# Both 3x3 convolutions of a Mamba-and-residual-block kernel computed on pairs of rows, six products a tile in place of nine

## The chip, the cores and the metric

The kernel runs on one core of a Trainium2 chip. The metric is device time in microseconds (us) of one launch. Before the change three runs gave 27951.63 us (median), 27945.47 and 27972.2. The profile is of one further execution, which took 27950.59 us, with a span of 27948.8 us from its first to its last instruction.

## The reference

Input `x` has 8 images of 64 channels and 128 x 128 points, in float32. Layer 0 runs a two-way Mamba block over all rows and over all columns, averages the two, normalises in groups, and adds `x`. Layer 1 is a residual block with two 3x3 convolutions whose weights are a mixture:

```
# layer 0
xr = run_bidir(rows of x); xc = run_bidir(columns of x)
x1 = silu(group_norm(0.5 * (xr + xc))) + x
# layer 1
w1 = (origin[0:K] + einsum('i,if->f', new_param, P[:, 0:K])).reshape(64, 64, 3, 3)
c1 = relu(batchnorm(conv3x3(x1, w1)))            # batch norm over all 8 images
w2 = (new_param[39] * origin[K:2K] + einsum(... P[:, K:2K])).reshape(64, 64, 3, 3)
out = relu(batchnorm(conv3x3(c1, w2)) + x1)
```

Both batch norms need the statistics of the whole batch before one point can be normalised, so the work falls into three parts with a hard border between them.

## The kernel before

**Layout.** An image lies on 128 partitions as two halves: partitions 0 to 63 hold the 64 channels of rows 0 to 63, partitions 64 to 127 those of rows 64 to 127. A tile is N = 512 points, 4 rows (`SEQ`) of both halves; an image has NT = 16 tiles.

**Part 1, the Mamba loop** (lines 511 to 576) is recorded by hand (`manual_schedule`): each engine's order is the order of the calls. It has 512 groups (8 images, 32 row groups and then 32 column groups each) of 16 slots; `s` counts slots, `n` groups, `r` is the slot in the group, and n % 64 the place in the image. Each slot has a scan on DVE (lines 368 and 370), a product with `c` on POOL (line 375), a drive product on DVE or, in 5 of 16 slots, POOL (line 360), and PE's products `pb` (340) and `yp` (391). Four generators are advanced by one step at fixed slots: `prepare` (the next group), `emit`, `normalize` (421 to 438) and `conv1` (453 to 478).

`normalize` handles an image in the 16 groups after it: a piece of 512 points a group, in slots 5 and 7. For a piece ACT takes the Silu, SP loads `xr`, POOL adds, and SP stores to `x1_d`.

`conv1` reads `x1_d` back. `strip_of` loads a strip of 6 rows on all 128 partitions into one of two buffers, for the tile after the one in work. A tile has nine products of a 128 x 128 weight, which holds the same 64 x 64 block for both halves and zeros elsewhere. It has five steps: three products in each of slots 14, 15 and 0, then in slot 1 the copy out of PSUM (ACT) and the store to `c1_d` (SP), and in slot 2 the statistics (DVE). The first strip is asked for in slot 12 of the group with n % 64 = 4, two slots ahead of its products. The tiles go 1 to 15 and then 0, since tile 0 needs the last row of the other half. The last image has no group after it, so the rest of `normalize` and then the whole of `conv1` run by themselves after the loop (lines 573 to 576):

```
for _ in norm:
    pass
for _ in conv3:
    pass
```

SP is one queue in order: it issues nearly all loads and stores, and an instruction that waits holds up those behind it.

**Part 2, the second convolution** (lines 586 to 636) is placed by the scheduler of the Tile layer. First it clears two image buffers (622), joins the statistics (593) and forms scale and shift. For each image four pieces of 16 rows are loaded to `ct` (ACT's queue), and ACT writes relu(scale x + shift) into `xp` (632). `halo` copies one row each way between the halves by DMA (600, 601), and 8 pairs of tiles of 2 x 9 products each follow (610), with statistics (614), a copy (616) and a store to `c2_d` (617).

**Part 3** (lines 643 to 651) adds `x1` to the normalised result and writes `out`.

Ahead of all this, lines 153 to 160 lay the mixed weights into `w1` and `w2s` with two DMAs each; `w2s` goes to `w2_d`, and only then do the first loads of the image (line 220) start.

Of the kernel before, what the change touches and what calls it, by code (L numbers as in the profile page):

```python
# [32 lines left out]
def tile_mamba2d_then_resblock(ctx: ExitStack, tc: tile.TileContext, x, par, gn, p_w, o_w, new_p, bn, cst, out):  # L33
# [10 lines left out]
    w2_d = dram.tile([P, 9, P], F32, name="w2_d")  # L44
# [12 lines left out]
    w1 = const.tile([P, 9, P], F32, name="w1")  # L57
# [6 lines left out]
    with tc.tile_pool(name="prep", bufs=2) as prep, tc.tile_pool(name="prep_ps", bufs=2, space=PSUM) as prep_ps:  # L64
# [88 lines left out]
        w2s = prep.tile([P, 9, P], F32, name="w2s", bufs=1)  # L153
        for k, w in enumerate((w1, w2s)):
            nc.vector.memset(w, 0.0)
            for hf in range(2):
                nc.sync.dma_start(
                    out=w[hf * C : (hf + 1) * C, :, hf * C : (hf + 1) * C], in_=wacc[k * C : (k + 1) * C]
                )
# [36 lines left out]
    with ExitStack() as st:  # L196
# [12 lines left out]
        for k in range(2):  # L209
            strip = big.tile([P, SEQ + 2, W + 2], F32, name=f"strip{k}")  # L210
            nc.vector.memset(strip, 0.0)
            strips.append(strip)
# [227 lines left out]
        def strip_of(b, t):  # L440
            x1 = x1_d[b].rearrange("p (h w) -> p h w", w=W)
            strip = strips[t % 2]
            lo, hi = max(SEQ * t - 1, 0), min(SEQ * (t + 1) + 1, HH)
            nc.sync.dma_start(out=strip[:, lo - SEQ * t + 1 : hi - SEQ * t + 1, 1 : W + 1], in_=x1[:, lo:hi, :])

            if t == 0:
                nc.vector.memset(strip[0:C, 0, :], 0.0)
                nc.sync.dma_start(out=strip[C:P, 0, 1 : W + 1], in_=x1[0:C, HH - 1, :])
            if t == NT - 1:
                nc.vector.memset(strip[C:P, SEQ + 1, :], 0.0)  # L450
                nc.sync.dma_start(out=strip[0:C, SEQ + 1, 1 : W + 1], in_=x1[C:P, 0, :])

        def conv1(b):


            strip_of(b, 1)
            st1 = small.tile([P, NT, 6], F32, name="st1", bufs=1)
            yield
            for t in [*range(1, NT), 0]:
                if t:  # L460
                    strip_of(b, (t + 1) % NT)
                ps = psm.tile([P, 2, N], F32, name="cps", tag="pt")[:, 0, :]
                for k in range(9):
                    kh, kw = divmod(k, 3)
                    nc.tensor.matmul(  # L465
                        ps.rearrange("p (r w) -> p r w", w=W), w1[:, k, :],
                        strips[t % 2][:, kh : kh + SEQ, kw : kw + W], start=(k == 0), stop=(k == 8),
                    )
                    if k % 3 == 2:
                        yield  # L470
                cs = work.tile([P, N], F32, name="cs", tag="tok", bufs=3)
                nc.scalar.copy(cs, ps)
                nc.sync.dma_start(out=c1_d[b][:, t * N : (t + 1) * N], in_=cs)
                yield
                nc.vector.bn_stats(st1[:, t, :], cs)
                if t == 0:
                    nc.sync.dma_start(out=st1_d[:, b], in_=st1)
                yield
# [32 lines left out]
        with tc.manual_schedule():  # L511
# [10 lines left out]
            for s in range(total + UN):  # L522
# [23 lines left out]
                if r in CONV and n % PER > 4 or r >= CONV[0] and n % PER == 4:  # L546
                    next(conv3, None)
# [10 lines left out]
                if r == OUT and prev:  # L558
                    if n % PER == 4:
                        next(conv3, None)  # L560
# [12 lines left out]
            for _ in norm:  # L573
                pass
            for _ in conv3:
                pass


    with ExitStack() as st:
# [6 lines left out]
        w2 = big.tile([P, 9, P], F32, name="w2")  # L586
# [11 lines left out]
        def halo(xp):  # L598

            nc.sync.dma_start(out=xp[0:C, HH + 1, 1 : W + 1], in_=xp[C:P, 1, 1 : W + 1])  # L600
            nc.scalar.dma_start(out=xp[C:P, 0, 1 : W + 1], in_=xp[0:C, HH, 1 : W + 1])

        def conv3x3(xp, w, stats, dst):
            for t in range(0, NT, 2):
                ps = psw.tile([P, 2, N], F32, name="cps")
                for j in range(2):
                    for k in range(9):
                        kh, kw = divmod(k, 3)
                        r = SEQ * (t + j) + kh
                        nc.tensor.matmul(  # L610
                            ps[:, j, :].rearrange("p (r w) -> p r w", w=W), w[:, k, :],
                            xp[:, r : r + SEQ, kw : kw + W], start=(k == 0), stop=(k == 8),
                        )
                    nc.vector.bn_stats(stats[:, t + j, :], ps[:, j, :])  # L614
                cs = stage.tile([P, 2 * N], F32, name="cs")
                nc.scalar.copy(cs, ps.rearrange("p j n -> p (j n)"))
                nc.sync.dma_start(out=dst[:, t * N : (t + 2) * N], in_=cs)

        xps = []
        for k in range(2):  # L620
            xp = big.tile([P, HH + 2, W + 2], F32, name=f"xp{k}")
# [4 lines left out]
        for b in range(B):  # L626
            xp = xps[b % 2]
            cb = c1_d[b].rearrange("p (h w) -> p h w", w=W)
            for k in range(4):
                ct = stage.tile([P, RB, W], F32, name="ct")  # L630
                nc.scalar.dma_start(out=ct, in_=cb[:, k * RB : (k + 1) * RB, :])
                nc.scalar.activation(  # L632
                    xp[:, 1 + k * RB : 1 + (k + 1) * RB, 1 : W + 1], ct, AF.Relu, bias=t, scale=s
                )
            halo(xp)
            conv3x3(xp, w2, st2[:, b], c2_d[b])
# [76 lines left out]
```

## Time and profile before

Times in us from the span's start, as the profile has them.

| what | us |
|---|---|
| execution that was profiled | 27950.59 |
| its span | 27948.8 |
| first scan of part 1 starts | 120.77 |
| first piece of the last image's norm: POOL adds | 26437.03 |
| last piece of it is stored | 26511.19 |
| first product of its `conv1` | 26515.38 |
| last `c1_d` store issued | 26656.00 |
| first write into `xp` | 26682.85 |
| first product of part 2 | 26695.67 |
| first write of part 3's result, `cc`, on DVE | 27708.77 |

Over the whole span DVE is busy 93%, POOL 90%, PE 71% and ACT 66%. These shares are those of part 1, which is 95% of the span; part 2 and part 3 have other limits.

A line of the groups of instructions reads: line, engine, operation, output<-inputs, shape, count | busy us, mean ns of one | idle us of that engine just before, and what ended most of it. A float32 product is recorded as two instructions here: 8 x 16 x 9 = 1152 products stand as x2304.

### The profile page before, as it was taken

The numbers are of one execution on the slowest core, as the hardware profiler recorded it, in microseconds if no ns is written. First come the engines' busy times: TensorE is split into PE (matmuls) and PEld (weight loads), VectorE is DVE, ScalarE is ACT, GpSimd is POOL, SyncE is SP. The second block draws the span as 40 slices with busy tenths as digits, with TensorE's granted clock in tenths as the row PEclk, the third lists the DMA queues.
The fourth block names the chain that finished last, engine by engine and source line by source line (L and its number), as shares of the span: only waits on it lengthen the run. The fifth ranks groups of instructions, "written<-read, shape, count | busy, mean of one in ns | idle before, by whom it ended". The sixth has DMA issues, their size and how long they took to land. (4 is left out here: it accounts for less than half of the span.)

```text
span 27948.8 us, 235723 instructions
## 1 busy us (share of the span) xinstructions
PE 19978.3 (71%) x66604; PEld 7011.9 (25%) x66604; DVE 26017.8 (93%) x16145; ACT 18328.2 (66%) x30622; POOL 25127.4 (90%) x10916
## 2 busy tenths in 40 slices
PE   6666677666876677666776667766786667766696
PEld 1122222222222222222222222222222222222232
DVE  8999999999999999999999999999999999999811
ACT  5666666666666666666666666666666666666511
POOL 7999999999999999999999999999999999999800
PEclk8888888888988888888888888888898888888798
DMA  5555555555555555555555555555555555555424
GB/s 177 177 174 169 181 185 181 172 169 180 193 176 171 171 184 188 176 168 180 182 184 174 169 182 186 179 172 170 183 191 176 170 175 183 187 177 170 160 81 164
DMA packets 1817540, 4880.91 MB, mean 175 GB/s; under 512 B 236688, under 2 KB 335648, under 8 KB 1799840
## 3 DMA queue, kind: packets, MB, share of 16 engines
q1 hardware_dynamic: 1796144, 4763.96, 51.3%
q10 hardware_dynamic: 15472, 68.32, 0.7%
q0 software_dynamic: 4608, 33.56, 0.3%
q8 instruction: 525, 8.60, 0.1%
q14 instruction: 791, 6.48, 0.1%
HBM read 4124.63 MB, written 739.18 MB: 174 GB/s over the span
## 5 line engine op out<-in xcount | busy, mean ns | idle before, releaser
L375 POOL TENSOR_TENSOR s<-s,c 128x1024 f32<-128x1024 f32 x8192 | 19117.8, 2364 | 1008.3 <-DVE s L370 354.7
L351 ACT ACTIVATE dA<-dl,A 128x508 f32<-128x508 f32 x16384 | 11275.1, 688 | 568.4 <-DMA dl<-dd 52.6
L340 PE MATMUL pb<-u,wb 128*128 128x512 f32 x8192 | 5396.9, 746 | 7362.9 <-DVE s L360 7019.2
L370 DVE TENSOR_TENSOR_SCAN s<-dA,s 128x1024 f32<-128x1024 f32 x4096 | 9295.8, 2280 | 53.9 <-ACT dA L351 40.6
L368 DVE TENSOR_TENSOR_SCAN s<-dA,s 128x1024 f32<-128x1024 f32 x4096 | 9286.9, 2278 | 0.0
L360 DVE TENSOR_TENSOR s<-du,pb 128x1024 f32<-128x1024 f32 x5632 | 6757.1, 1200 | 473.8 <-DMA du<-dd 338.3
L360 POOL TENSOR_TENSOR s<-du,bt 128x1024 f32<-128x1024 f32 x2560 | 6054.9, 2365 | 326.7 <-DMA bt<-bd 127.9
L348 ACT COPY dA<-zeros 128x8 f32<-128x8 f32 x8192 | 1349.0, 165 | 6284.0 <-DVE s L370 4603.6
L391 PE MATMUL yp<-s,fold 128*32 128x512 f32 x32768 | 5388.8, 672 | 5.1 <-POOL s L375 5.1
L340 PEld LDWEIGHTS pb<-u,wb 128*128 128x128 f32 x8192 | 1483.3, 216 | 10217.8 <-DVE s L360 5203.8
L234 PE MATMUL cp<-xc,wc 128*128 128x256 f32 (+3 forms) x8192 | 2151.1, 408 | 0.0
L228 PE MATMUL cp<-xt,wc 128*128 128x512 f32 (+3 forms) x4096 | 2026.2, 618 | 73.7 <-DMA xt<-x_h 73.5
L234 PEld LDWEIGHTS cp<-xc,wc 128*128 128x128 f32 x8192 | 1647.6, 207 | 1071.8 <-issue 459.6
L391 PEld LDWEIGHTS yp<-s,fold 128*32 128x32 f32 x32768 | 820.1, 114 | 3438.6 <-issue 1923.5
L288 PE MATMUL bp<-u,xpT 128*32 128x512 f32 x2048 | 1632.3, 947 | 4.8 <-ACT dl L282 4.8
L351 ACT ACT_TABLE_LOAD x1030 | 1321.5, 1283 | 21.4 <-DMA dl<-dd 3.5
L651 POOL DMA_DIRECT2D out<-cc x32 | 17.2, 537 | 1414.7 <-ACT cc L650 1414.7
L465 PE MATMUL cps<-strip,w 128*128 128x512 f32 x2304 | 1077.2, 606 | 170.7 <-DMA strip<-x_d 160.5
L228 PEld LDWEIGHTS cp<-xt,wc 128*128 128x128 f32 x4096 | 768.7, 198 | 1377.1 <-issue 1089.7
L266 PE MATMUL dp<-u,wd 128*128 128x512 f32 x2048 | 1035.9, 631 | 1.2 <-ACT u L259 1.2
L610 PE MATMUL cps<-xp,w 128*128 128x512 f32 x2304 | 1004.2, 596 | 17.0 <-DMA xp<-xp 16.2
L292 ACT COPY bc<-bp 32x1024 f32<-32x1024 f32 x512 | 513.0, 1002 | 740.4 <-PE yp L391 709.8
(106 smaller groups left out, 10679.9 us busy)
## 6 DMA issues: line engine op xcount, KB each, us to landing
c<-bd SPq DMA_DIRECT2D x2049, 512.0 KB, 4.7
dl<-dd SPq DMA_DIRECT2D x2048, 512.0 KB, 6.4
du<-dd SPq DMA_DIRECT2D x2048, 512.0 KB, 7.3
bt<-bd SPq DMA_DIRECT2D x2560, 256.0 KB, 4.7
dd<-du SPq DMA_DIRECT2D x2048, 128.0 KB, 2.3
dd<-dl SPq DMA_DIRECT2D x2048, 128.0 KB, 2.4
bd<-bc SPq DMA_DIRECT2D x512, 128.0 KB, 5.4
strip<-x_d SPq DMA_DIRECT2D x112, 384.0 KB, 9.5
```

Source lines behind the costliest of these rows:

```text
L228: nc.tensor.matmul(ps[:, :, lo:hi], lhsT[hf], xt[:, r : r + SEQ, lo - s : hi - s], start=start, stop=stop)
L234: nc.tensor.matmul(ps[:, :, lo:hi], lhsT[hf], g["xc"][:, :, lo - s - hf * HH : hi - s - hf * HH], start=start and hf == 0, stop=stop and h ...
L288: nc.tensor.matmul(bp[0 : 2 * NS, d, :], w["wbc"], u[:, d, :], start=True, stop=True)
L340: nc.tensor.matmul(pb, wt[g["o"]]["wb"][:, P * ng : P * (ng + 1)], g["u"][:, d, :], start=True, stop=True)
L348: nc.scalar.copy(dA[:, :, :, edge], zeros)
L351: nc.scalar.activation(dA[:, j, :, t], dl[:, j, :, t], AF.Exp, scale=wt[g["o"]]["A"][:, 2 * half + j, ng : ng + 1])
L360: engine.tensor_mul(s, g["du", half, d], b.unsqueeze(1).to_broadcast([P, 2, N]))
L368: nc.vector.tensor_tensor_scan(s, a, s, 0.0, ALU.mult, ALU.add)
L370: nc.vector.tensor_tensor_scan(s[:, ::-1], a[:, ::-1], s[:, ::-1], 0.0, ALU.mult, ALU.add)
L375: nc.gpsimd.tensor_mul(s, s, c.unsqueeze(1).to_broadcast([P, 2, N]))
L391: nc.tensor.matmul(g["yp"][32 * q : 32 * (q + 1), :], fold, s[:, j, :], start=False, stop=r == UN - 2, skip_group_check=True,)
L465: nc.tensor.matmul(ps.rearrange("p (r w) -> p r w", w=W), w1[:, k, :], strips[t % 2][:, kh : kh + SEQ, kw : kw + W], start=(k == 0), stop= ...
```

## The change

Both convolutions now work on pairs of rows: partitions 0 to 63 hold the even row of each pair and partitions 64 to 127 the odd row, for the output; for the input the two lie one row apart. An output pair then needs two input pairs (`blk` 0 and 1) and three shifts across (`kw`): six products, with three of the four 64 x 64 blocks of each weight in use.

The weights are laid by six DMAs each in place of two. A strip is 5 rows on each half of the partitions, taken from every second row of `x1_d`, by two DMAs (three where the rows cross from one half of the image to the other). `conv1` starts one group later (n % 64 = 5), takes the tiles in an order that follows the pieces of the norm, and does two products in each of its three steps. For the last image five pieces of the norm come first, then one piece and one tile in turn. In part 2 `halo` is gone; `xp` has 65 rows, the first and the last piece are written in halves of 64 partitions, and the result is put back into the old layout by two stores for each pair of tiles, in runs of one row.

```diff
-        w2s = prep.tile([P, 9, P], F32, name="w2s", bufs=1)
+        w2s = prep.tile([P, 2, 3, P], F32, name="w2s", bufs=1)
         for k, w in enumerate((w1, w2s)):
             nc.vector.memset(w, 0.0)
-            for hf in range(2):
-                nc.sync.dma_start(
-                    out=w[hf * C : (hf + 1) * C, :, hf * C : (hf + 1) * C], in_=wacc[k * C : (k + 1) * C]
-                )
+            for blk in range(2):
+                for e in range(2):
+                    for m in range(2):
+                        kh = 2 * blk - e - m + 1
+                        if 0 <= kh < 3:
+                            nc.sync.dma_start(
+                                out=w[e * C : (e + 1) * C, blk, :, m * C : (m + 1) * C],
+                                in_=wacc[k * C : (k + 1) * C, 3 * kh : 3 * kh + 3, :],
+                            )
...
-        def strip_of(b, t):
+        def strip_of(b, t, k):
...
+            for e in range(2):
+                es = slice(e * C, (e + 1) * C)
+                rows = [2 * SEQ * t + 2 * j - e for j in range(SEQ + 1)]
+                for hf in range(2):
+                    js = [j for j, r in enumerate(rows) if hf * HH <= r < (hf + 1) * HH]
+                    if js:
+                        r = rows[js[0]] - hf * HH
+                        nc.sync.dma_start(
+                            out=strip[es, js[0] : js[-1] + 1, 1 : W + 1],
+                            in_=x1[hf * C : (hf + 1) * C, r : r + 2 * len(js) - 1 : 2, :],
+                        )
...
-            strip_of(b, 1)
+            order = [0, 1, 9, 2, 10, 3, 11, 4, 12, 5, 13, 6, 14, 7, 15, 8]
+            strip_of(b, order[0], 0)
...
-            for t in [*range(1, NT), 0]:
-                if t:
-                    strip_of(b, (t + 1) % NT)
+            for k, t in enumerate(order):
+                if k + 1 < NT:
+                    strip_of(b, order[k + 1], k + 1)
...
-                for k in range(9):
...
+                for kw in range(3):
+                    for blk in range(2):
+                        nc.tensor.matmul(
+                            ps.rearrange("p (r w) -> p r w", w=W), w1[:, blk, kw, :],
+                            strips[k % 2][:, blk : blk + SEQ, kw : kw + W],
+                            start=(kw == 0 and blk == 0), stop=(kw == 2 and blk == 1),
+                        )
+                    yield
...
-                if r in CONV and n % PER > 4 or r >= CONV[0] and n % PER == 4:
+                if r in CONV and n % PER > 5 or r >= CONV[0] and n % PER == 5:
                     next(conv3, None)
...
-            for _ in norm:
-                pass
-            for _ in conv3:
-                pass
+            for _ in range(2 * 5):
+                next(norm)
+            next(conv3)
+            for _ in range(NT):
+                for _ in range(2):
+                    next(norm, None)
+                for _ in range(5):
+                    next(conv3)
...
-            for k in range(4):
+            for k in range(0, HH + 1, RB):
                 ct = stage.tile([P, RB, W], F32, name="ct")
-                nc.scalar.dma_start(out=ct, in_=cb[:, k * RB : (k + 1) * RB, :])
...
+                for e in range(2):
+                    es = slice(e * C, (e + 1) * C)
+                    lo, hi = max(k, e), min(k + RB, HH + e)
+                    if lo < hi:
+                        nc.scalar.dma_start(out=ct[es, lo - k : hi - k, :], in_=cb[es, lo - e : hi - e, :])
+                        if k == 0 or k == HH:
+                            nc.scalar.activation(
+                                xp[es, lo:hi, 1 : W + 1], ct[es, lo - k : hi - k, :], AF.Relu, bias=t[es], scale=s[es]
+                            )
+                if 0 < k < HH:
+                    nc.scalar.activation(xp[:, k : k + RB, 1 : W + 1], ct, AF.Relu, bias=t, scale=s)
-            halo(xp)
-            conv3x3(xp, w2, st2[:, b], c2_d[b])
+            for k in range(0, NT, 2):
+                ps = psw.tile([P, 2, N], F32, name="cps")
+                for j in range(2):
+                    for kw in range(3):
+                        for blk in range(2):
+                            r = SEQ * (k + j) + blk
+                            nc.tensor.matmul(
+                                ps[:, j, :].rearrange("p (r w) -> p r w", w=W), w2[:, blk, kw, :],
+                                xp[:, r : r + SEQ, kw : kw + W],
+                                start=(kw == 0 and blk == 0), stop=(kw == 2 and blk == 1),
+                            )
...
+                hf, j0 = divmod(SEQ * k, HH // 2)
+                for e in range(2):
+                    nc.sync.dma_start(
+                        out=c2v[hf, :, j0 : j0 + 2 * SEQ, e, :],
+                        in_=cs[e * C : (e + 1) * C].rearrange("p (j w) -> p j w", w=W),
+                    )
```

## The prediction

> **What bounds the kernel now.** I read the chain that ended last first. It is followed back only to 26665 us, so it says nothing of part 1, but it shows what part 2 is made of: one unbroken run of products, from the halo copy to the statistics.
>
> ```profile
> 26682.85 2.45 ACT xp L632 x2
> 26685.30 1.53 issue
> 26686.83 0.13 ACT xp L632
> 26686.96 6.35 DMA ct<-c_d
> 26693.31 0.02 issue
> 26693.33 0.02 ACT xp L632
> 26693.36 0.32 issue
> 26693.67 1.86 DMA xp<-xp
> 26695.53 0.14 issue
> 26695.67 996.22 PE cps L610 x2286
> ```
>
> Each row is start, us, what. The last row is PE's, 0.436 us a record (996.22 / 2286), and the rows above it are the way there: relu pieces, a late `ct` load, the halo copy. The groups of instructions confirm it, and show where the first convolution stands:
>
> ```profile
> L465 PE MATMUL cps<-strip,w 128*128 128x512 f32 x2304 | 1077.2, 606 | 170.7 <-DMA strip<-x_d 160.5 <-ACT cs L472 10.3
> L610 PE MATMUL cps<-xp,w 128*128 128x512 f32 x2304 | 1004.2, 596 | 17.0 <-DMA xp<-xp 16.2 <-DVE st L614 0.8
> ```
>
> L610 is busy 1004.2 us and idle 17.0, of which 16.2 came before the first product: part 2 is PE's alone. L465 waited 160.5 us for strips, in 8 waits (list of waits): one for each image, 81.3 us of it for the last image, which waits for its norm; the other seven take 79.2 us, 11.3 each.
>
> Part 1 is not PE's. In the table by stretches, groups of the second image without convolution or norm (4473.29 to 5028.11) have DVE busy 541.41 of 554.82 us and POOL 534.67. The timelines of one first strip show the exception:
>
> ```profile
> 3628.21 1.12 PE L340 MATMUL pb<-u,wb 128*128 128x512 f32 x2 [0.68 <-ACT sz L303]
> 3639.86 4.37 PE L465 MATMUL cps<-strip,w 128*128 128x512 f32 x6 [10.53 <-DMA strip<-x_d]
> 3644.16 1.07 PE L391 MATMUL yp<-s,fold 128*32 128x512 f32 x8
> 3645.16 2.84 PE L465 MATMUL cps<-strip,w 128*128 128x512 f32 x6
> 3647.84 1.02 PE L340 MATMUL pb<-u,wb 128*128 128x512 f32 x2
> 3648.69 2.74 PE L465 MATMUL cps<-strip,w 128*128 128x512 f32 x6
> ```
>
> PE stands 10.53 us before the first product; `pb` is behind it, and DVE waits 9.82 us for that `pb` and 2.33 for the next (its timeline), 12.15 for the image.
>
> The tail of part 1, the last image alone, is two chains in a row. SP's timeline (the last two norm pieces, then the first strips) and PE's:
>
> ```profile
> 26506.62 0.32 SPq L437 DMA_DIRECT2D x_d<-xr  x1
> 26507.03 0.38 SPq L434 DMA_DIRECT2D xr<-x_h  x1
> 26511.19 0.32 SPq L437 DMA_DIRECT2D x_d<-xr  x1
> 26511.56 1.10 SPq L444 DMA_DIRECT2D strip<-x_d  x2
> ...
> 26515.38 9.82 PE L465 MATMUL cps<-strip,w 128*128 128x512 f32 x18 [81.26 <-DMA strip<-x_d]
> 26525.92 7.99 PE L465 MATMUL cps<-strip,w 128*128 128x512 f32 x18 [0.72 <-ACT cs L472]
> ```
>
> A store waits for its add and holds the next load back; the strips come when the last piece is out, and only then does PE start.
>
> **The change, part by part.**
>
> *Second convolution, products.* 8 x 16 x 6 x 2 = 1536 records in place of 2304, at the measured 0.436 us (1004.2 / 2304): **-334.7**. A product has the same 512 columns and its own weight load, so its price stays. Is PE still last? A pair of tiles will take 24 x 0.436 = 10.5 us. DVE needs 2 x 0.70 (L614). ACT needs 1.01 (L616) and an eighth of an image's pieces; 3 full ones at 2.10, two of 64 partitions with as many elements, one of a row: about 10.7 / 8 = 1.3. The ten loads of `ct` add some 0.4 us of issue each, 0.5 a pair; 2.9 in all. If ACT also stood out the 4.9 us to landing of each of five pieces it would be 6.0. SP's two stores of 256 KB move in runs of 512 bytes. No such store is in the trace; the nearest row is the strip load, 384 KB in pieces of 512 bytes, which came 3.8 us after its issue in the quiet tail. Two stores in 10.5 us fit; below zero there is nothing to gain, so 0.
>
> *Way into part 2.* The first product now needs only the first piece of `xp`, two half-partition writes of 2.1 and 2.0 us after 26682.85, 4.1 us, where it took 12.8 (26695.67 less 26682.85): **-8.7**. The halo's DMAs were on that path and go; nothing replaces them.
>
> *Tail of part 1.* Before: norm to 26511.19, strip, then 16 tiles, last store at 26656.00. A norm piece takes 4.7 us (SP issues `xr`, POOL adds 3.0 after that, 1.26, SP stores and issues the next); a tile takes 8.67 (7.99 and 0.68 for the copy, as PSUM has one buffer here). After: five pieces, stored by 26459.8 as before; two strips issued from 26460.1; first product 3.8 later. The first tile takes 12 x 0.444 = 5.3 and 1.8 for a cold start (9.82 against 7.99 now), its store is at 26471.7. From then on SP holds, in order, load of piece k+5, its store, two strip loads for tile k+1, store of tile k. So a load of `xr` waits for the tile before, and a strip for the add: 0.4 + 3.0 + 1.3 + 0.4 (store) + 0.4 + 3.6 (two strips, landing) + 5.3 + 0.7 = 15.1 us. The strip it fetches is for the tile after next, so 15.1 us bring two tiles: 7.55 each. Ten tiles to 26547.2, then five without norm at 5.3 + 0.7 = 6.0: 26577.2. Against 26656.0: **-78.8**. Everything from there to 26682.85 (clearing, joining statistics) keeps its length; 65 rows for 66 give 0.2. The new order moves `ct` loads behind the last copy on ACT's queue, but 27 us of DVE hide their landing.
>
> [...] The row: the granted clock was 0.50 in 26450 to 26500, with PE idle, and 1.00 from 26550 (table by stretches); the first tile took 1.8 us more than the next. [...] In the 15.1 us PE is idle 15.1 - 10.7 = 4.4, once 0.7 and once 3.7. [...] I take 0 and keep 10 for the range.
>
> *First strips of the other seven images.* These stay: still asked for in slot 12, used in slot 14. A second strip DMA is issued 0.6 us later (rows of SP near 3632): +0.6. But the products in the way of the two late `pb` shrink by a third: 4.37, 2.84 and 2.74 give back 1.5 + 0.9 + 0.9. -2.7 an image, **-19** for seven.
>
> *Other convolution groups.* By the stretches of the second to fourth image, norm groups with convolution (places 6 to 16) take 52.01, 51.69 and 52.20 us, without it (2 to 4) 51.65, 52.12 and 51.68; places 17 to 20 take 51.01, 51.16 and 51.31, later ones 50.44, 50.47 and 50.27. So convolution costs 0.15 and 0.77 a group, 11 x 0.15 + 4 x 0.77 = 4.7 an image, 33 for seven. PE's third of it would be 11; but SP gets one more issue of 0.6 us in slot 14, ahead of a `bt` load; behind stand the next slots' loads of `c`, for which POOL waits (284.7 us over the span), and the `c1_d` store, which waits for ACT anyway. If that issue came through in full: 112 x 0.6 = +67; if convolution became free, -33. I take **-4**, nearer to the row of POOL and ACT, which PE does not touch.
>
> *Weights.* SP now issues 12 small DMAs where 4 took 2.74 us (0.69 each), and the first image load waits for what follows them: 8 x 0.65 = **+5**. Before 89.44 nothing covers it.
>
> *Part 3* reads and writes what it did: 0.
>
> Sum: -334.7 - 8.7 - 78.8 - 0.2 - 19 - 4 + 5 = -440. On the profiled execution, 27950.6 - 440 = 27510.6; the median of the runs shown lies 1.0 higher, so **27512**.
>
> **Rivals.**
>
> *Tail one after the other* (8%). If the strip comes only for the very next tile, as a wait on the newest store to `x1_d` would make it, each of 11 tiles costs the whole 15.1: +83, the tail gains nothing, 27595. Against: at 26511.56 the old first strip was issued 0.37 after the last piece's store began; it did not wait for that store.
>
> *Another engine takes over part 2* (7%). ACT's loads and writes are in one order with its copies. If they take 12.5 us a pair in place of 10.5, 64 pairs add 130: 27640. For: ACT stood up to 13.9 us for PE in part 2 (list of waits). Against: 2.9 to 6.0 us of work in 10.5.
>
> *First strips hidden or convolution free* (4%): 12.15 - 2.7 = 9.5 more for each of seven images, about -66: 27446. Nothing in the order speaks for it.
>
> *Slower* (3%). Place: PE's queue in slot 14 of every convolution group. If two strip DMAs behind busy loads landed after their slot, every tile would stand as the first does now. Price: 9.5 us (12.15 - 2.7) x 105 further tiles = +997, 28510. It decides from 440 / 112 = 3.9 us a group. For: PE does stand 11.3 us at each first strip. Against: all later strips are asked for a whole group, 51 us, ahead, and land after 9.5 (list of DMA issues).
>
> That the change does not do what it says: six products a tile are in the text, so PE's records must fall; no chance kept.
>
> **How the numbers follow.** 78% for the forecast. Its own bounds: tail +10 for cold starts and some 10 for landings, groups -29 to +71 around my -4, weights 2 less. These do not all fall together, so 27475 to 27575; it holds nearly all of the 78% and, by the first rival's smaller forms, a few more. A change under 0.2% (56 us) cannot be told from none here. Faster 0.96, within 0.2% 0.01, slower 0.03.
>
> **What would show it.** Part 2's products with x1536, about 670 us, idle before the first about 8. `xp` to the first product 4 us. Last `c1_d` store some 140 us after the last norm starts (26437.03), not 219. Waits of PE for strips near 80 us for seven images. Groups of places 6 to 20 within 0.5 us of now. The forecast is wrong if part 2's products show gaps, or if DVE's waits for `pb` grow.

## The result, and the profile after

The changed kernel takes **27639.19 us** (median; 27638.15 to 27651.24), against 27948.74 for the kernel before in the same runs: 309.6 us less, a ratio of 0.9888 with a 95% interval of 0.9871 to 0.9906. The profiled execution took 27638.15 us, its span is 27636.0. The forecast was 27512, with 27575 as its upper end.

The groups of instructions on which the account rests (line, engine, operation, tiles | busy us, mean ns | idle us before them, and what ended it). First two of the kernel before, then three of the changed one:

```profile
L360 DVE TENSOR_TENSOR s<-du,pb 128x1024 f32<-128x1024 f32 x5632 | 6757.1, 1200 | 473.8 <-DMA du<-dd 338.3 <-PE pb L340 103.5 <-PE cp L228 14.0
L375 POOL TENSOR_TENSOR s<-s,c 128x1024 f32<-128x1024 f32 x8192 | 19117.8, 2364 | 1008.3 <-DVE s L370 354.7 <-DVE s L360 320.4 <-DMA c<-bd 284.7
```

```profile
L481 PE MATMUL cps<-strip,w 128*128 128x512 f32 x1536 | 754.4, 618 | 134.3 <-DMA strip<-x_d 128.0
L367 DVE TENSOR_TENSOR s<-du,pb 128x1024 f32<-128x1024 f32 x5632 | 6757.8, 1200 | 559.0 <-DMA du<-dd 452.1
L382 POOL TENSOR_TENSOR s<-s,c 128x1024 f32<-128x1024 f32 x8192 | 19121.0, 2364 | 1104.3 <-DMA c<-bd 440.6
```

The first of these three (line 465 before: 1077.2 us, x2304) has lost a third of its products and some 320 us of busy time; it is the work that the change was made on. The other two are groups that the change does not touch at all, and they tell where time went. DVE's drive products (line 360 before, 367 now) stood 559.0 us where they stood 473.8, and the part ended by a load of `du` rose from 338.3 to 452.1. POOL's wait for `c` (375 before, 382 now) rose from 284.7 to 440.6.

The table by stretches says where. The columns of a row are the stretch, its length, busy time (and records) of PE, PE's weight loads, DVE, ACT and POOL, the granted clock, DMA's share and GB/s. The stretch is places 8 to 16 of the fifth image (a place is the number of a group in its image), nine groups with a piece of the norm and a tile of the convolution each. First the kernel before, then the changed one:

```profile
13684.62:14154.24 469.62, 373.07 (x1170) 119.46 (x1169) 449.58 (x271) 325.52 (x550) 449.77 (x199) 0.90 0.58 192
```

```profile
13715.07:14196.26 481.19, 358.10 (x1116) 109.97 (x1116) 450.03 (x271) 325.45 (x550) 449.95 (x199) 0.89 0.58 186
```

DVE, ACT and POOL do the same work to within half a us; PE does 15 us less; and the stretch is 11.6 us longer. Over seven images such a group takes 53.44 us instead of 52.11, and one of places 17 to 20 takes 51.72 instead of 51.02; later ones are as before (50.25 and 51.24, against 50.35 and 51.21). These groups do less arithmetic and take longer.

The sum, term by term, between two points that both traces have:

| step of the prediction | forecast | measured | from |
|---|---|---|---|
| weights | +5 | +3.9 | first scan, 120.77 to 124.71 |
| first strips, seven images | -19 | -18.3 | the group with the stall, 63.60 to 60.98 |
| other convolution groups | -4 | **+108.1** | places 5, 7 to 20 of seven images |
| rest of the loop | 0 | -5.5 | what is left up to the tail |
| tail | -78.8 | -71.3 | first add to last `c1_d` store, 219.0 to 147.7 |
| way into part 2 | -8.9 | -4.4 | that store to the first product, 39.67 to 35.24 |
| products of part 2 | -334.7 | -328.95 | 1005.01 to 676.06 |
| part 3 | 0 | +3.7 | last product to the end, 248.1 to 251.8 |
| sum | -440 | -312.8 | spans, 27948.8 to 27636.0 |

### The profile page after: what moved, and what is told of

Same layout as the page of the kernel before. It is cut to its first block, busy times and chain, and to the rows that moved or that the text cites. A ratio compares the mean times of both kernels' runs of the same rounds, so it can differ in the third digit from the quotient of the medians.

```text
span 27636.0 us, 232983 instructions
## 1 busy us (share of the span) xinstructions
PE 19347.3 (70%) x65068; PEld 6675.0 (24%) x65068; DVE 26018.6 (94%) x16145; ACT 18349.8 (66%) x30638; POOL 25128.0 (91%) x10916
## 4 chain that ended last, share of the span: by engine, by line
DVE 40%; issue 21%; PE 17%; DMA 10%; ACT 8%; POOL 2%; SPq 1%; DVEq 0%; POOLq 0%; ACTq 0%
DVE s L367 14%; DVE s L375 12%; DVE s L377 10%; DMA du<-dd 7%; PE pb L347 6%; ACT dA L358 4%; PE yp L398 3%; PE cps L650 2%; PE dp L273 2%; PE bp L295 2%; DVE du L287 2%; POOL s L382 1%; DVE y L405 1%; DMA bt<-bd 1%; PE cp L241 1%
## 5 line engine op out<-in xcount | busy, mean ns | idle before, releaser
L382 POOL TENSOR_TENSOR s<-s,c 128x1024 f32<-128x1024 f32 x8192 | 19121.0, 2364 | 1104.3 <-DMA c<-bd 440.6
L367 DVE TENSOR_TENSOR s<-du,pb 128x1024 f32<-128x1024 f32 x5632 | 6757.8, 1200 | 559.0 <-DMA du<-dd 452.1
L241 PE MATMUL cp<-xc,wc 128*128 128x256 f32 (+3 forms) x8192 | 2095.3, 401 | 0.0
L388 PE MATMUL yp<-u,dg 128*128 128x512 f32 x2048 | 961.9, 592 | 1.2 <-DVE y L405 1.2
L481 PE MATMUL cps<-strip,w 128*128 128x512 f32 x1536 | 754.4, 618 | 134.3 <-DMA strip<-x_d 128.0
```

The costliest lines, as they stand in the source:

```text
L241: nc.tensor.matmul(ps[:, :, lo:hi], lhsT[hf], g["xc"][:, :, lo - s - hf * HH : hi - s - hf * HH], start=start and hf == 0, stop=stop and h ...
L367: engine.tensor_mul(s, g["du", half, d], b.unsqueeze(1).to_broadcast([P, 2, N]))
L382: nc.gpsimd.tensor_mul(s, s, c.unsqueeze(1).to_broadcast([P, 2, N]))
```

## The experiments

### What slows the groups

All kernels below but the last two were run once each, and the kernel before, run beside them, took between 27936 and 28022 us. So a total is read to some tens of us, and the argument is carried by the groups (means of 63, in places 8 to 16 of seven images) and by single rows of the traces.

Three theories at first. **A**: the strip's second load is one more issue in SP's queue, which shifts the loads behind it. **B**: its traffic is worse than that of the old strip and slows other loads. **C**: fewer products change PE's timing, and with it the order in which things fall due.

`x1_one_issue` does not load the upper half of the strip; `x2_tiny` issues both loads, of one row each. First the edit of the one, then that of the other:

```diff
-                    if js:
+                    if js and e == 0:
```

```diff
-                    js = [j for j, r in enumerate(rows) if hf * HH <= r < (hf + 1) * HH]
+                    js = [j for j, r in enumerate(rows) if hf * HH <= r < (hf + 1) * HH][:1]
...
-                            in_=x1[hf * C : (hf + 1) * C, r : r + 2 * len(js) - 1 : 2, :],
+                            in_=x1[hf * C : (hf + 1) * C, r : r + 1, :]
```

> The changed kernel, but the strip's half for partitions 64 to 127 is never loaded (that half stays zero), so each strip is one load on SP's queue in place of two, with half the bytes. Read by groups at places 8 to 17 of images 1 to 7 (53.1 us in the changed kernel, 51.9 at places 7 to 16 before). Theory A (the second load on SP's queue[...] makes the du loads late): 51.9, DVE's wait for du back to 1.7 a group. Theory B (the traffic of the row-strided half strips slows the du loads): half of the loss left, 52.5. Theory C (three products fewer change when the other pieces of a group come): 53.1, as in the changed kernel.

> The changed kernel, but each strip load brings one row only (the other rows keep what is in the buffer), so that SP issues as many loads as the changed kernel and the bytes of a strip fall to a fifth. Groups at places 8 to 17: theory A (number of issues) 53.1; theory B (traffic) 51.9 to 52.1; theory C (fewer products) 53.1.

`x1_one_issue` took 27615.76 us, groups 8 to 16 at 52.91: 0.8 of the loss of 1.33 us is left, with half the bytes and one load a strip. `x2_tiny` took 27528.99, those groups at 52.22, DVE's wait for `du` in them at 1.80 us a group (3.11 in the changed kernel, 1.64 before). All issues are there, the loss is not. A falls, B stands.

`x3_before_six` is the kernel before with three of nine products left out; `x4_hybrid` keeps the old first convolution and takes only the new second one, which then reads every second row of the old layout. The main line of the former's edit (the end of the sum and the steps follow it):

```diff
-                for k in range(9):
+                for k in range(6):
...
```

> The kernel before, with the three products of the lowest row of the filter left out of the first convolution: six products a tile in three steps of two, strips and loads as before. Groups at places 7 to 16: theories A and B 51.9 or a little less, DVE's wait for du 1.7 a group; theory C (fewer products) 53.1. The stall at the first strip of an image should shrink from about 11.5 to about 9 us.

> First convolution, its order, its strips and the tail of part 1 as before the change; part 2 as changed, with each row piece loaded from the old layout. All theories: groups at places 7 to 16 at 51.9, last group starts near 26373 us as before, part 2 at 676 us, in all 27948.7 less 329 (products of part 2) less 4 to 8 (way into it): 27612 to 27616. If the loss in part 1 came from anything that part 2 does (it cannot by time, but the pools and orders differ), it would be near 27700.

`x3_before_six` took 27912.33, groups 8 to 16 at 52.05, the one with the first strip at 60.2 instead of 63.6. So C falls, and the 2.7 us an image that I took for the shorter wait of `pb` is seen by itself (3.4). `x4_hybrid` took 27624.96, groups 8 to 16 at 52.12: the loss belongs to the new first convolution, and it eats what that convolution gains at the first strips and in the tail: without it the kernel took 14 us less than the changed one, which one run cannot tell from nothing.

What makes fewer bytes worse traffic? The DMA records of the trace have the time of each packet. The 512-byte packets of a strip took 27.6 ns on average before and 47.6 in the changed kernel, 36.2 in `x1_one_issue` and 27.3 in `x2_tiny`. Two things are new in these loads: every second row of the source (**S**), and two loads of 64 partitions in place of one of 128 (**P**). `x5_contig` is the changed kernel with neighbouring rows; `x6_before_split` is the kernel before with its strip in two loads:

```diff
-                            in_=x1[hf * C : (hf + 1) * C, r : r + 2 * len(js) - 1 : 2, :],
+                            in_=x1[hf * C : (hf + 1) * C, min(r, HH - len(js)) : min(r, HH - len(js)) + len(js), :],
```

```diff
-            nc.sync.dma_start(out=strip[:, ...], in_=x1[:, lo:hi, :])
+            for hs in (slice(0, C), slice(C, P)):
+                nc.sync.dma_start(out=strip[hs, ...], in_=x1[hs, lo:hi, :])
```

> The changed kernel, with one thing different: each half of the pair layout's strip is read as 5 neighbouring rows of the source instead of every second row (the products then work on other rows; sizes, number of loads and the 64-partition halves are as in the changed kernel). Theory S (the row stride at the source is what makes the strip's packets slow): 512-byte packets go back from 47.6 to about 28 ns, groups 8 to 16 of an image from 53.4 to about 52.1 us, the whole to about 27,535 us. Rival P (the split on 64 partitions a load is what slows them): packets stay near 47 ns, groups stay at 53.4 us, the whole at about 27,639 us.

> The kernel before, with each strip loaded by two loads of 64 partitions and 6 neighbouring rows, all 9 products kept. Theory S (row stride): packets stay near 28 ns, groups 8 to 16 stay at 52.1 us, the whole at about 27,949 us. Rival P (split on 64 partitions): packets near 47 ns, groups 8 to 16 at about 53.4 us, the whole some 80 to 100 us longer.

`x5_contig`: packets 47.3 ns, groups 8 to 16 at 53.32, 27665.44 in all. `x6_before_split`: packets **51.1 ns**, groups at **53.59**, 28100.68 in all, 120 above the median of the kernel before beside it (27980.22 in seven runs, the slowest 28021.63). Nothing else was changed in it: same rows, same bytes, nine products. Places 8 to 16 of the fifth image:

```profile
13742.86:14224.87 482.01, 378.17 (x1172) 120.61 (x1171) 449.98 (x271) 325.22 (x550) 449.24 (x199) 0.90 0.59 186
```

482.01 us, where the kernel before has 469.62, by this alone. S falls, P stands. The number of loads is not all of it, since `x1_one_issue` has one load a strip, of 64 partitions, and is slow too; two loads of all 128 partitions, each of half the rows, were not run. The opposite test is one load of 128 partitions in the changed kernel, in `x8_one128` with the memsets of the edge rows and in `x11_one128_clean` without (the edit shown).

```diff
+            lo = min(2 * SEQ * (t % (NT // 2)), HH - SEQ - 1)
+            nc.sync.dma_start(out=strip[:, :, 1 : W + 1], in_=x1[:, lo : lo + SEQ + 1, :])
-            for e in range(2):
+            for e in range(0):
...
```

> The changed kernel, with each strip of the pair layout read by one load of 128 partitions and 5 neighbouring rows (so the products work on other rows; bytes as in the changed kernel, one load instead of two). Theory P (the split in loads of 64 partitions is what slows the packets): 512-byte packets back from 47.6 to about 27.6 ns, groups 8 to 16 from 53.4 to about 52.1 us, the wait for du in them from 3.1 to about 1.7 us, the whole about 100 us shorter than the changed kernel, near 27,540 us. Rival Q (fewer rows of a strip, or where the pair order of the tiles puts the loads, is what delays du): packets may be fast, but groups stay at 53.4 us and the whole at about 27,640 us.

> x8_one128 without the two memsets of an edge row in each image (the load does not leave that row free any more, so that VectorE waited for it). Theory P (the split in loads of 64 partitions): groups 8 to 16 stay at about 52.2 us, places 17 to 20 go back to about 51.0, the group with the stall of the first strip stays near 62 us, and the last group starts about 90 us earlier than in the changed kernel, the whole at about 27,550 us. Rival Q (the loads' place delays du whatever their width): 17 to 20 stay above 51.7 us and the whole near 27,640 us.

`x8_one128`: packets 27.3 ns and groups 8 to 16 at 52.26, but 27673.14 in all. The one load also writes the edge row that a memset on DVE clears, so twice an image DVE stood for a strip, 15.2 and 11.7 us on average (the groups in places 5 and 18 took 67.93 and 62.81). `x11_one128_clean`, without these memsets, took 27596.9: groups 8 to 16 at 52.31, 17 to 20 at 51.06, last group 59.5 us earlier than in the changed kernel. The stretch again:

```profile
13707.29:14174.37 467.08, 354.25 (x1116) 109.19 (x1116) 449.14 (x272) 326.87 (x550) 449.63 (x199) 0.90 0.57 191
```

467.08 with six products and as many bytes as in the changed kernel. Places 8 to 20 give back 63 x 1.13 + 28 x 0.66 = 90 us. That only 59.5 of these show at the last group is within what the loop moves by itself: three kernels here with the same loop (but for a third strip buffer in one) start their last group at 26461.9, 26476.5 and 26502.7. Part 3 then took 273.6 us here, 21.8 more than in the changed kernel with the same code, so that the total is only 42 lower.

Over all traces the groups of places 8 to 16 fall into two classes: 52.05 to 52.31 us in the eight kernels whose strip is one load of 128 partitions or a row at a time, 53.32 to 53.59 in the five with two full loads of 64, and `x1_one_issue` between them.

**How it gets to DVE.** Who waited in the stretch, us in total, times, longest (list of waits). The kernel before, the changed one, `x6_before_split`:

```profile
DVE s L360 <- DMA du<-dd: 14.2, 9, 2.5
POOL s L375 <- DMA c<-bd: 12.7, 8, 2.1
```

```profile
DVE s L367 <- DMA du<-dd: 27.4, 11, 5.0
POOL s L382 <- DMA c<-bd: 25.4, 9, 3.9
```

```profile
DVE s L360 <- DMA du<-dd: 21.8, 10, 5.1
POOL s L375 <- DMA c<-bd: 27.6, 9, 3.9
```

DVE's wait has grown by 13.2 us, the stretch by 11.6. The way there is in SP's loads of places 8 to 16, by issue and landing (medians): in the changed kernel the first `c` load of a group lands 8.2 us after its issue (5.9 before, 6.2 in `x11_one128_clean`) and the second `bt` load 8.4 (6.2; 6.4). They are issued 4.9 and 5.6 us into the group, and the strip's packets run from 5.5 to 10.0 us (4.9 to 8.2 before). POOL waits for that `c` (2.8 us a group, 1.0 before), the next `c` load waits for POOL and is issued 21.1 us into the group in place of 19.4, and everything behind it on SP moves along: the `dd` stores, and the last `du` load, at 51.6 in place of 49.4. DVE needs that `du` in the next group and waits. `x6_before_split` has the same picture (8.8, 8.4, 21.4, 51.6).

### The tail

In the changed kernel the last image's tiles ran like this (PE's timeline; in brackets the idle time before):

```profile
26557.21 5.42 PE L481 MATMUL cps<-strip,w 128*128 128x512 f32 x12 [0.72 <-ACT cs L488]
26566.48 7.09 PE L481 MATMUL cps<-strip,w 128*128 128x512 f32 x12 [3.85 <-DMA strip<-x_d]
26574.29 5.42 PE L481 MATMUL cps<-strip,w 128*128 128x512 f32 x12 [0.72 <-ACT cs L488]
26584.02 7.00 PE L481 MATMUL cps<-strip,w 128*128 128x512 f32 x12 [4.31 <-DMA strip<-x_d]
```

Every second tile is 1.6 us slower, and it is the one that waited. `x9_three` takes the waits away from some tiles: a third buffer, and in the last image a strip is asked for two tiles ahead.

```diff
-        for k in range(2):
+        for k in range(3):
             strip = big.tile(...)
...
-                if k + 1 < NT:
-                    strip_of(b, order[k + 1], k + 1)
+                last = b == B - 1
+                if k == 0 and last:
+                    strip_of(b, order[1], 1)
+                d = k + 1 + last
+                if d < NT:
+                    strip_of(b, order[d], d)
...
-                            strips[k % 2][:, blk : blk + SEQ, kw : kw + W],
+                            strips[k % 3][:, blk : blk + SEQ, kw : kw + W],
```

> The changed kernel with a third strip buffer; in the last image each strip is asked for two tiles ahead instead of one. Computes the same. Clock theory (every second tile of the tail is slow, 7.09 instead of 5.42 us, because TensorE stood idle 3.6 to 4.3 us before it): without those waits all tiles take about 5.42 us, a tile's cycle goes from a mean of 8.4 to about 6.2 us, and the tail from 147.7 to about 112 us. Rival (the slow tiles come from the strips' write or from their place in the pair): the waits go but every second tile still takes about 7.1 us, tail about 125 us. Rival (the norm's pieces set the pace): waits stay, tail stays near 148 us.

```profile
26610.40 5.42 PE L485 MATMUL cps<-strip,w 128*128 128x512 f32 x12 [0.72 <-ACT cs L492]
26616.54 5.42 PE L485 MATMUL cps<-strip,w 128*128 128x512 f32 x12 [0.72 <-ACT cs L492]
26625.20 6.82 PE L485 MATMUL cps<-strip,w 128*128 128x512 f32 x12 [3.24 <-DMA strip<-x_d]
26632.92 5.39 PE L485 MATMUL cps<-strip,w 128*128 128x512 f32 x12 [0.91 <-DMA strip<-x_d]
```

Where the wait is gone, two tiles in a row take 5.42; where it came back (3.24 us) the tile takes 6.82. The nine tiles with 3.2 to 4.3 us of idle time before them, in the two tails, took 6.8 to 7.1 us, and none with under 1 us took over 5.42. So a slow tile needs a wait. The length of the wait does not settle it, though, as two tiles of `x10_ct_small` show (a kernel of the next section with the same code in the tail):

```profile
26582.33 5.39 PE L481 MATMUL cps<-strip,w 128*128 128x512 f32 x12 [3.57 <-DMA strip<-x_d]
26589.75 7.08 PE L481 MATMUL cps<-strip,w 128*128 128x512 f32 x12 [2.03 <-DMA strip<-x_d]
```

A wait of 3.57 us, and the tile is fast; one of 2.03, and it is slow. The granted clock tells why: in the traces it changes only on a grid of 3.413 us (each stretch at one clock, but for a trace's last, is a whole number of such windows). Here are five windows of the grid in a row, by the table by stretches:

```profile
26577.18:26580.59 3.41, 1.58 (x4) 0.38 (x2) 0.69 (x1) 1.30 (x2) 0.73 (x1) 1.00 0.41 127
26580.59:26584.00 3.41, 1.68 (x4) 0.86 (x5) 0.00 (x0) 0.00 (x0) 0.00 (x0) 1.00 0.65 200
26584.00:26587.42 3.42, 3.42 (x9) 1.32 (x7) 0.00 (x0) 0.00 (x0) 1.27 (x1) 1.00 0.24 83
26587.42:26590.83 3.41, 1.38 (x4) 0.63 (x4) 0.69 (x1) 1.30 (x2) 0.00 (x0) 1.00 0.75 234
26590.83:26594.25 3.42, 3.42 (x6) 1.36 (x5) 0.00 (x0) 0.00 (x0) 1.26 (x1) 0.50 0.08 32
```

The border of two windows cuts the long wait, so that PE is busy 1.58 and 1.68 us in them, and the clock stays at 1.00. The short wait lies in one window, with PE busy 1.38 us, and the next window has 0.50. The eight tails with this order of tiles (the changed kernel, `x1_one_issue`, `x2_tiny`, `x5_contig`, `x8_one128` to `x11_one128_clean`) have 120 tiles after their first ones. All 27 whose wait filled 0.58 or more of one window ran slow, none of the 89 whose wait filled less than 0.545 of any, and two of the four between.

But my 112 us for the tail was a miss: it took 140.9 (147.7 in the changed kernel). After the head start is used up a piece of the norm comes every 7.5 to 9.2 us, and the strips wait for the pieces: that rival was right too. (27674.18 us in all; the loop before the tail was 40.8 us later than in the changed kernel, where the edit changes only which buffer a strip goes to.)

### The way into part 2

The changed kernel from the last copy on (rows of the timeline of all engines):

```profile
26672.58 6.89 ACTq L636 DMA_DIRECT2D ct<-c_d  x6
26672.90 0.32 SPq L489 DMA_DIRECT2D c_d<-cs  x1
26674.14 7.10 DVE L623 MEMSET xp<- 128x8450 f32 x1 [6.63 <-issue]
26681.16 0.64 DVE L491 BATCH_NORM_STATS2 st<-cs 128x6 f32<-128x512 f32 x1
26681.82 0.32 SPq L493 DMA_DIRECT2D st_d<-st  x1
26691.95 0.32 SPq L612 DMA_DIRECT2D st<-st_d  x1
26694.98 3.62 DVE L614 BATCH_NORM_AGGREGATE mv<-st 128x2 f32<-128x768 f32 x1 [4.38 <-DMA st<-st_d]
```

The statistics go out at 26681.82 and are read back only at 26691.95, 10.1 us later; the chain of waits gives that store a row of 10.11 us, while the other seven of its kind land in 1.5. DVE stood 4.38 us for it. `x10_ct_small` makes the six early `ct` loads small:

```diff
                     lo, hi = max(k, e), min(k + RB, HH + e)
+                    if b == 0:
+                        hi = min(hi, lo + 1)
...
```

> The changed kernel with image 0's part of the second convolution loading and copying only the first row of each piece (the rest of that image's input stays zero). If the six early ct loads are what delays the landing of the statistics: st_d lands in about 1.5 us instead of 10.1, the wait of bn_aggr for st (4.38 us) goes, and it starts behind the second memset, some 4 us earlier after the last c1_d store. Rival (the store of the statistics is slow at this place for another reason): the landing stays near 10 us. The rest of the kernel at about 27,639 us less some 8 us of shorter copies.

```profile
26694.82 0.32 SPq L493 DMA_DIRECT2D st_d<-st  x1
26699.84 0.32 SPq L612 DMA_DIRECT2D st<-st_d  x1
26703.52 3.56 DVE L614 BATCH_NORM_AGGREGATE mv<-st 128x2 f32<-128x768 f32 x1
```

The store lands in 5.0 us, not 10.1, and DVE's wait is gone. That it is not 1.5 may be due to three `xx` loads issued ahead of it, where the changed kernel has one; this was not tried. What the joining now waits for is DVE's second memset, and the statistics are joined 17.6 us after the last `c1_d` store instead of 22.1. So these loads are the cause of the wait. (27651.49 us in all, the last group 14.6 later than in the changed kernel.)

### A faster version

No run so far combines what the tests left standing: whole strips, a first strip in time, the short tail, the new second convolution. `x7_best` is `x4_hybrid` with the first strip asked for in slot 8 in place of 12, and the last image's norm and tiles in turn, at nine products a tile.

```diff
+                if r == 8 and prev and n % PER == 4:
+                    next(conv3, None)
...
-                    if n % PER == 4:
-                        next(conv3, None)
...
-            for _ in norm:
-                pass
-            for _ in conv3:
-                pass
+            for _ in range(2 * 4):
+                next(norm)
+            next(conv3)
+            for _ in range(NT):
+                for _ in range(2):
+                    next(norm, None)
+                for _ in range(5):
+                    next(conv3)
```

> The kernel before with the new second convolution alone (27,625 us as a run before), its first strip of an image asked for in slot 8 of the group instead of slot 12, and the last image's norm and first convolution in turn, still on 9 products a tile. If the group in place 5 waits only for its first strip and an earlier request moves that landing ahead of the need: place 5 falls from 63 to about 52 us, some 75 us over seven images; the tail falls from 219 to about 166 us; whole about 27,495 us. Rival: the earlier strip delays the du loads of the group before (as the second half strip did), place 4 or 5 grows by as much as is saved: about 27,570 us.

It took **27533.07 us** (median of 4) against 27980.22 before in that batch, a ratio of 0.984 (0.9824 to 0.9856), below the changed kernel's interval. The group with the first strip, place 5, takes 52.71 us (63.09 in `x4_hybrid`), and place 4, where the strip is now asked for, 52.98 (52.00): the rival holds for a tenth of what is saved. The tail takes 161.5 us. These two steps brought 73 and 57 us, where I had worked out 75 and 53. The total is 38 above my figure; of this 22 lie in the rest of the loop, 7 of them in place 4, and 11 in parts 2 and 3, where `x4_hybrid` has the same code.

`x12_best_edges` adds one thing, seen in the last timeline of the changed kernel: the last statistics stand behind a memset of a whole image buffer.

```diff
-            nc.vector.memset(xp, 0.0)
+            for edge in (xp[:, :, 0:1], xp[:, :, W + 1 : W + 2], xp[:, 0:1, :], xp[:, HH : HH + 1, :]):
+                nc.vector.memset(edge, 0.0)
```

> x7_best with the two 7.10 us memsets of the whole padded image at the start of the second convolution cut down to its edges. In x7_best the last bn_stats of the first convolution stands behind one of these memsets. If that wait is on the path: from the last c1_d store to the first product some 7 to 12 us less, and nothing else changed: about 27,522 us. Rival: another wait (the landing of the early ct loads or of the statistics) is late next, and nothing or little is gained: about 27,530 us.

From the last `c1_d` store to the first product it takes 26.10 us, where `x7_best` takes 37.35: 11.25 less, as expected. 8.2 of these are the memset that no longer stands before the last statistics; the rest is a quicker way of these out and back, with three `ct` loads issued ahead of them in place of seven. The total, **27503.79 us**, ratio 0.9835 (0.9819 to 0.9852), cannot be told from that of `x7_best` by its interval; 18 us of the difference lie in the loop, where the edit changes nothing.

## Why the prediction was right and wrong

**Products of part 2: right.** PE is the bound before and after, and no engine took over.

```profile
26708.14:27384.20 676.06, 675.25 (x1536) 285.79 (x1536) 88.77 (x127) 144.15 (x109) 0.00 (x0) 1.00 0.41 100
```

675.25 us of 676.06 are PE's. The size was 5.8 too large: the 0.436 us a record is a mean that holds some 17 us of fixed time (the products start at a granted clock of 0.50, in 26695 to 26698 before and 26706 to 26710 after, and there are short gaps), which does not shrink with the count: an estimate, 1005.01 less 2304 x 0.429, and 676.06 less 1536 x 0.429. Records start 0.429 us apart in both kernels, and 768 x 0.429 = 329.5, 0.5 from what was measured.

**The failed step: "Other convolution groups", taken at -4, measured +108.** I priced the second strip DMA as an issue on SP (0.6 us, +67 at most) and PE's part as a gain. The time of the issue costs nothing that can be seen (`x2_tiny`, groups 8 to 16 at 52.22 us), and PE's work neither (`x3_before_six`, 52.05; 52.11 before). What I did not price at all was what the load does while it is in flight: two loads of 64 partitions with five sixths of the bytes of the old strip keep its packets 1.7 times as long (47.6 ns for 27.6), the `c` and `bt` loads next to them land 2.2 to 2.3 us later, and POOL and then DVE wait for it. The runs show this from both sides: the split alone costs the old kernel 1.48 us a group in places 8 to 16, and the unsplit load gives the new one 1.13 back. My reason for -4, "nearer to the row of POOL and ACT, which PE does not touch", looked at who computes, in a stage where loads of `du` already ended 338 of DVE's 474 us of idle time.

The packets took 27.6 ns in one load of 128 partitions, 47.6 in the changed kernel's two loads of 64 and 51.1 in those of `x6_before_split` (x 1.72 and 1.85). The single load of 64 in `x1_one_issue` has 36.2, only x 1.31, and two loads of 64 with one row each (`x2_tiny`) have 27.3. What in the hardware lengthens the packets is not shown by these runs, nor why the single load has less.

**First strips: right**, -18.3 for -19, and for the reason given (`x3_before_six`).

**Tail: mechanism right, size 7.5 short.** Strips do come two tiles at a time, but the cycle is 17.0 us and not 15.1: every second tile began at half clock (0.50 in 26568.0 to 26570.0, against 1.00 in 26574.0 to 26580.0), +1.6, and the two issues take 1.26 us, not 0.8. For such starts I had kept 10 us in the range (5.5 times the 1.8 us of the first tile) and taken 0, on an estimate that 3.7 us of idle time would seldom be enough. The tail before could not show that: its first tile, 9.82 us, came after 81.26 us of idle time, and the other fifteen, 7.99 each, after 0.7. In the changed kernel the five waits of 3.56 to 4.31 us all brought a slow tile, and over the eight tails 0.58 of a window was enough, in 27 of 27 tiles. So +10 was the better price. That it came due at every one of the five waits is partly luck: the cycle of 17.0 us is close to five windows (17.07), so each wait met its window at nearly the same place; in `x10_ct_small` two of four waits of 3.6 to 3.7 us passed without a slow tile.

**Way into part 2: half of it.** The halo's path did go. But "27 us of DVE hide their landing" asked only whether the `ct` loads come in time, not what they delay: the store of the statistics, on the path, was issued at 26681.82, while packets of ACT's queue (six `ct` loads and an `xx` load behind them) ran from 26674.6 to 26692.6; its own packets ran only from 26687.7 to 26691.1, and it landed after 10.1 us instead of 1.5 (5.0 in `x10_ct_small`). DVE's wait of 4.4 us for it took half of the gain back.

**Weights** 1.1 less than forecast. **Part 3** is 3.7 us longer, which says nothing: in the eight kernels with the changed kernel's code for it, it takes between 251.4 and 273.6 us.

The forecast's marks had it right that waits of PE for strips stay small (82 us for seven images), and wrong that the groups of places 6 to 20 stay within 0.5 us. Its sign of being wrong looked at the wrong row: DVE's waits for `pb` fell, from 103.5 to 83.9 us, and those for `du` grew.

## What to carry to other kernels

When a change cuts a load into parts, price it in flight, not at its issue: look up what else is loaded in those microseconds and who waits for that, above all where the stage's idle time is already ended by DMAs (338.3 of 473.8 us before DVE's drive products here). If a load's neighbours are needed soon, try it on all 128 partitions: here that took 27.3 to 27.6 ns a packet and 52.05 to 52.31 us a group, where two full loads of 64 took 47.3 to 51.1 ns and 53.32 to 53.59 us. A layout that halves the partitions of each load cost more here than it gave to the first convolution: 108.1 us in the groups, against 89.6 at the first strips and in the tail. And a transfer that comes early enough for its own reader may still hold up a small one on the path, as the `ct` loads did with the store of the statistics (10.1 us instead of 1.5).

## What the runs showed of the hardware

- Packets of 512 bytes took 27.6 ns in a load of 128 partitions (27.3 in `x8_one128`) and 47.3 to 51.1 in two loads of 64 with 5 or 6 rows, whether the source rows were neighbours (47.3 in `x5_contig`, 51.1 in `x6_before_split`) or every second one (47.6 in the changed kernel). The stride over rows cost nothing that can be seen. A single load of 64 had 36.2 (`x1_one_issue`), two of one row each 27.3 (`x2_tiny`).
- Others pay too: packets of 2048 bytes in the same groups went from 97.2 to 102.7 ns, while in later groups, which have no strips (places 24 to 31), they are alike in both kernels (104.3 and 105.1).
- The granted clock changed only on a grid of 3.413 us. In the eight tails with this order of tiles a tile ran slow (6.8 to 7.1 us in place of 5.42) when the wait before it filled 0.58 or more of one window of that grid (27 of 27), and not when it filled less than 0.545 of any (0 of 89). So a wait of 1.89 us could bring a slow tile, and one of 3.69 us none (both in `x10_ct_small`).
- A store of 48 KB that lands in 1.5 us elsewhere took 10.1 us with six `ct` loads issued ahead of it (the changed kernel), and 5.0 with these cut to a row each (`x10_ct_small`).
